# A two-layer graph and expert kernel on one core: the first layer's expert blocks get their first product from seven half-size products as well, alternating with the second product of the block before

## The chip, the cores and the metric

One core of a Trainium2 chip runs the whole program. The metric is the device time of one execution in microseconds (us); the time of a kernel is the median of its runs. TensorE (PE in the profile; PEld is its loading of weights) multiplies, VectorE (DVE), ScalarE (ACT) and GpSimd (POOL) work on tiles, SyncE (SP) issues most of the loads from HBM. Each engine takes its own instructions in order and waits on semaphores for the others.

## The reference

Two layers, each a graph step followed by a mixture of eight experts of which two are taken for each of 3327 tokens with 256 features. The change touches the experts of the first layer only:

```python
def _L0_ffn_ref(x, Wg, bg, W1, b1, W2, b2):
    B, S, D, H, E, K = (8, 8192, 256, 1024, 8, 2)
    gate_scores = jnp.einsum('bsd,ed->bse', x, Wg) + bg
    topk_scores, topk_idx = jax.lax.top_k(gate_scores, K)
    topk_probs = jax.nn.softmax(topk_scores, axis=-1)
    combine = jnp.sum(topk_probs[..., None] * jax.nn.one_hot(topk_idx, E, dtype=x.dtype), axis=-2)
    out = jnp.zeros_like(x)
    for e in range(E):
        h = jax.nn.relu(jnp.einsum('bsd,hd->bsh', x, W1[e]) + b1[e])
        y = jnp.einsum('bsh,dh->bsd', h, W2[e]) + b2[e]
        out = out + combine[..., e:e + 1] * y
    return out
...
x = x + _L0_gnn_ref(_layernorm(x, axis=-1), adj, L0_gnn_W, L0_gnn_b)
x = x + _L0_ffn_ref((_layernorm(x, axis=-1))[None], L0_ffn_Wg, L0_ffn_bg, L0_ffn_W1, L0_ffn_b1, L0_ffn_W2, L0_ffn_b2)[0]
```

All of it is in float32.

## The kernel before

Tokens are sorted by expert into a list in HBM (`xlist0`), each row with its weight and its place. The experts work on this list in blocks that belong to one expert each: `step` handles block t. A usual block has 256 rows (two groups of 128); blocks 12, 17, 22, 27 and a few at the end have 128. Blocks 0 to 7 are planned early; 8 to 29 are always run. Three blocks fit into the six places of the ring in SBUF, two places each: w1, the rows (`xb`) and b1 in the one, w2 and b2 in the other.

What step t does before the change:

- `load` issues the loads of block t+2 on SP, in the order `xlist`, w1 (L1296), b1, w2, b2. The first waits until the place of block t-1 is free, that is until VectorE has done the last L1434 of that block (it reads the rows' weights from `xb`).
- `prepare` has VectorE make four sums of quarters of w2 (L1346 to L1349, 128x512 each) in the tile `gate`.
- `first` computes the hidden tile hT of 1024 x 256 from xT, the block turned to features by rows, and w1: for each of eight chunks of 128 hidden features two matmuls of 128x256 (L1379) into a PSUM bank of pool `psh`, then one ScalarE activation, relu with the bias (L1387).
- `weighed_bias` fills y with the bias by the row's weight (ScalarE, L1364). `turned` transposes block t+1 on TensorE (L1325) and ScalarE copies it (L1329).
- `second_seven` (blocks 3 to 28 of 256 rows) computes the second product as seven products of half-size blocks in place of eight: VectorE makes four sums of quarters of hT (L1370, L1418 to L1420), TensorE multiplies four 128x128 matmuls for each of the seven (L1427), VectorE adds each result, by the row's weight, into the quarters of y it belongs to (L1434), and GpSimd scatters the two halves of y to HBM (L946). The 128-row blocks use `second` (L1476, L1483, L1484).

All matmuls of a block's first product come before those of its second. Which instruction stands where in an engine's queue is decided by a scheduler when the program is built, from the order in the code; within an engine the order is then fixed.

The kernel's PSUM tiles come from three pools: two buffers in `psh`, four in `psy` (second products), two in `pst` (transposes elsewhere in the kernel). `xn` is a work tile with three buffers, used when tokens are routed and between the layers. Elsewhere in the kernel, while the second layer's graph step runs, GpSimd adds tiles of 128x512 in SBUF (L1870) and copies them (L919) while VectorE adds larger tiles (L459) and, from PSUM, L717.

Of the kernel before, what the change touches and what calls it, by code (L numbers as in the profile page):

```python
# [10 lines left out]
F32 = mybir.dt.float32  # L11
# [11 lines left out]
P = 128  # L23
NT = 26
NP = NT * P
D = 256
# [102 lines left out]
def gnn_moe_two_layers(  # L129
# [1086 lines left out]
    def experts(xlist, ys, group, fixed, n_hidden, func, w1T, b1, w2T, b2, copy, order_of_places, kept=None,  # L1216
                seven=None):

# [113 lines left out]
        def halves(a, k, i):  # L1332
            return a[:, k * hc_n // 2 : (k + 1) * hc_n // 2, ts(i, P)]

        def prepare(t):

            if not seven or t not in seven or groups_of(t) < SG:
                return None
            w2 = loaded[t][4]
            flat = gate.rearrange("p e d -> p (e d)")  # L1340
            n = hc_n // 2 * P
            sums = [flat[:, i * n : (i + 1) * n].rearrange("p (c d) -> p c d", d=P) for i in range(4)]
            t1, t3, t2, t4 = sums
            b21, b22 = halves(w2, 1, 0), halves(w2, 1, 1)
            with behind(last_y):
                nc.vector.tensor_tensor(t1, halves(w2, 0, 1), halves(w2, 0, 0), ALU.subtract)  # L1346
                nc.vector.tensor_tensor(t2, b22, t1, ALU.subtract)
                nc.vector.tensor_tensor(t4, b21, t2, ALU.subtract)
                nc.vector.tensor_tensor(t3, b22, halves(w2, 0, 1), ALU.subtract)  # L1349
            tokens_ = [  # L1350
                work.tile([P, DC, 2 * P], F32, name=name, bufs=2).rearrange(
                    "p c (h d) -> p (c h) d", d=P
                )
                for name in ("xnT", "xnT", "h2T", "h2T")
            ]
            return sums, tokens_

# [53 lines left out]
        def second_seven(t, late, hT, sums, y):  # L1411

            (t1, t3, t2, t4), (s1, s2, s3, s4) = sums
            _, xb, _, _, w2, _ = loaded[t]
            index = place_of(t, late)
            a11, a12, a21, a22 = (halves(hT, k, i) for i in range(2) for k in range(2))
            b11, b21, b22 = halves(w2, 0, 0), halves(w2, 1, 0), halves(w2, 1, 1)
            nc.vector.tensor_tensor(s1, a21, a22, ALU.add)  # L1418
            nc.vector.tensor_tensor(s2, s1, a11, ALU.subtract)
            nc.vector.tensor_tensor(s4, a12, s2, ALU.subtract)  # L1420
            ps_x, ps_q, ps_b, ps_z = (
                psy.tile([P, P], F32, name="ps_y", tag="py") for _ in range(4)
            )

# [12 lines left out]

            multiply(ps_x, a11, b11)
            put_in(0, 0, ps_x)
            multiply(ps_q, a22, t4)  # L1440
            put_in(1, 0, ps_q)
            multiply(ps_b, a12, b21)
            put_in(0, 0, ps_b)
            multiply(ps_z, s1, t1)
            put_in(1, 1, ps_z)
            multiply(ps_x, s2, t2, False)
            put_in(0, 1, ps_x)
            multiply(ps_z, s4, b22, False)
            put_in(0, 1, ps_z)
            put(y, index, 0)  # L1450
            multiply(ps_x, s3, t3, False)
            put_in(1, 0, ps_x)
            put_in(1, 1, ps_x)
            put(y, index, 1)

# [47 lines left out]
        def step(late, end=always, place=None, between=None):  # L1503
# [3 lines left out]
            while len(loaded) < min(t + RING // places, end):  # L1507
                load(late)
            if t not in ready:
                ready[t] = turned(loaded[t][1], groups_of(t))  # L1510
# [136 lines left out]
    def count(pan, k, copied):  # L1647
# [9 lines left out]
        xlist0, ys0, "0", FIXED[0], H, AF.Relu, f0_w1T, f0_b1, f0_w2T, f0_b2,  # L1657
        nc.scalar.copy, BLOCKS0, seven=range(3, EARLY + LATE_PAIRS + FIXED[0] - 1),
    )

# [542 lines left out]
```

## Time and profile before

| what | value |
|---|---|
| median of 11 runs (lowest to highest) | 1171.19 us (1168.41 to 1174.14) |
| the profiled execution | 1169.44 us, span 1167.7 us |
| granted TensorE clock | 0.994 |
| TensorE busy, 0 to 200 us | 194.92 us |
| TensorE busy, 200 to 400 us | 200.00 us |
| TensorE busy, 1100 us to the end | 45.17 of 68 us |
| VectorE / ScalarE / GpSimd busy, 500 to 550 us | 24.80 / 18.47 / 7.34 of 50 us |
| first product L1379 x1184 | 253.4 us, 367 ns mean of one |
| second product of 256-row blocks, L1427, five rows of the page's groups | x352 46.5, x352 43.1, three x176 of 23.3 us |
| relu L1387 x282 | 128.5 us, 457 ns mean; 473 ns for 128x256 |
| VectorE sums L1418 x22, 128x512 | 692 ns mean |
| VectorE L1434 x176, 128x128 from PSUM | 348 ns mean |
| GpSimd sum L1870 x12, 128x512 | 1.26 to 4.52 us |

A float32 matmul has two records in the profile (the transposes have one). The records of matmuls that follow each other overlap in the trace (a mean of 367 ns for 1184 records, but 253.4 us busy), so the cost of a matmul is read from the distance between starts. In the page a group's idle time is that of its engine just before its instructions.

### The profile page before, as it was taken

What the parts mean: (1) busy time and instruction counts of PE and PEld (TensorE: products, weight loads), DVE (VectorE), ACT (ScalarE), POOL (GpSimd) and SP (SyncE); (2) the same over time, 40 slices, a digit from 0 to 9 for tenths busy, and PEclk for the clock granted to TensorE, in tenths of its full rate; (3) what the DMA queues carried; (4) which work ended last, traced back from release to release, by engine and by line L of the source; (5) the groups of instructions that cost most, each with busy time, mean ns of one, the idle gap of its engine ahead of it and who ended that gap; (6) DMA issues with size and microseconds to landing.
All of it is one profiled execution on the core that took longest, in us unless ns stands there. A gap on an engine that the chain in (4) does not pass through costs nothing. (4 is left out here: it accounts for less than half of the span.)

```text
span 1167.7 us, 19508 instructions
## 1 busy us (share of the span) xinstructions
PE 1136.4 (97%) x6235; PEld 995.0 (85%) x6235; DVE 838.1 (72%) x2621; ACT 606.0 (52%) x1111; POOL 317.0 (27%) x370
## 2 busy tenths in 40 slices
PE   8999999999999999999999999999999999999983
PEld 7888888888888888889898888888888888888872
DVE  6699999988885555454545569675897887886464
ACT  5689657550323333433333425997797776143331
POOL 2111331342431111111111110011353254465442
PEclk9999999999999999999999999999999999999997
DMA  9996638715467655766675856227347443478686
GB/s 350 189 292 244 234 131 250 260 58 185 141 223 236 222 197 185 246 210 204 206 253 186 318 192 266 85 92 252 129 148 265 165 144 136 144 249 243 223 300 228
DMA packets 123248, 241.68 MB, mean 207 GB/s; under 512 B 24528, under 2 KB 93184, under 8 KB 116224
## 3 DMA queue, kind: packets, MB, share of 16 engines
q1 hardware_dynamic: 108656, 205.59, 53.3%
q0 software_dynamic: 11200, 31.61, 7.4%
q10 hardware_dynamic: 3280, 3.15, 0.8%
q8 instruction: 51, 0.84, 0.3%
q14 instruction: 61, 0.50, 0.1%
HBM read 203.99 MB, written 36.33 MB: 206 GB/s over the span
## 5 line engine op out<-in xcount | busy, mean ns | idle before, releaser
L1387 ACT ACTIVATE pad<-ps_h,ring 128x256 f32<-128x256 f32 (+1 forms) x282 | 128.5, 457 | 284.6 <-PE ps_h L1379 149.6
L1379 PE MATMUL ps_h<-pad,ring 128*128 128x256 f32 (+1 forms) x1184 | 253.4, 367 | 3.1 <-ACT pad L1329 2.7
L1379 PEld LDWEIGHTS ps_h<-pad,ring 128*128 128x128 f32 x1184 | 200.6, 190 | 44.8 <-ACT pad L1387 10.3
L449 PE MATMUL ps_g<-ring,pad 128*128 128x256 f32 x1040 | 235.6, 381 | 0.8 <-DMA ring<-in_adjT 0.8
L449 PEld LDWEIGHTS ps_g<-ring,pad 128*128 128x128 f32 x1040 | 195.4, 190 | 26.0 <-DMA ring<-in_adjT 1.2
L946 POOL DMA_INDIRECT ys<-pad,index x114 | 115.7, 1015 | 361.8 <-DVE pad L1434 223.3
L449 PE MATMUL ps_g<-ring,s 128*128 128x256 f32 x780 | 176.9, 379 | 0.0
L459 DVE TENSOR_TENSOR ring<-ring,ring 128x768 f32<-128x768 f32 (+1 forms) x160 | 167.7, 1091 | 0.0
L449 PEld LDWEIGHTS ps_g<-ring,s 128*128 128x128 f32 x780 | 148.2, 190 | 19.6
L675 ACT ACTIVATE ring<-ring 128x3328 f32<-128x3328 f32 x54 | 160.0, 2976 | 1.4 <-DMA ring<-in_adjT 1.1
L946 POOL DMA_INDIRECT xlist<-xn,rt_idx x104 | 118.9, 1143 | 127.4 <-issue 30.0
L1651 ACT ACTIVATE sign<-ring,below 128x416 bf16<-128x416 f32 x208 | 133.4, 641 | 11.7 <-DMA ring<-in_adjT 5.7
L819 DVE SCALAR_TENSOR_TENSOR rt_product<-xn,gate 128x256 f32<-128x256 f32 x256 | 116.5, 455 | 15.0 <-ACT xn L361 6.2
L1434 DVE SCALAR_TENSOR_TENSOR pad<-ps_y,ring,pad 128x128 f32<-128x128 f32 x176 | 59.2, 348 | 47.3 <-PE ps_y L1427 47.2
L474 PE MATMUL ps_g<-ring,s 128*128 128x256 f32 x312 | 68.8, 380 | 3.2 <-ACT s L361 3.2
L474 PEld LDWEIGHTS ps_g<-ring,s 128*128 128x128 f32 x312 | 59.0, 190 | 11.7 <-ACT s L361 4.1
L756 PE MATMUL ps_g<-s,ring 128*128 128x256 f32 x312 | 69.0, 380 | 0.0
L756 PEld LDWEIGHTS ps_g<-s,ring 128*128 128x128 f32 x312 | 59.0, 191 | 7.7
L1418 DVE TENSOR_TENSOR xnT<-pad 128x512 f32<-128x512 f32 x22 | 15.2, 692 | 59.4 <-ACT pad L1387 59.4
L1476 PE MATMUL ps_y<-ring,pad 128*128 128x256 f32 x224 | 52.4, 380 | 0.0
L1476 PE MATMUL ps_y<-s,pad 128*128 128x256 f32 (+1 forms) x200 | 48.9, 383 | 0.1
L929 POOL COPY xn<-rt_w 128x4 f32<-128x4 f32 x26 | 4.5, 199 | 162.9 <-DVE rt_w L892 162.9
(255 smaller groups left out, 1566.2 us busy)
## 6 DMA issues: line engine op xcount, KB each, us to landing
ring<-in_adjT SPq DMA_DIRECT2D x50, 1664.0 KB, 8.1
ring<-in_f_w1T SPq DMA_DIRECT2D x30, 1024.0 KB, 6.9
ring<-in_f_w2T SPq DMA_DIRECT2D x30, 1024.0 KB, 7.5
ring<-xlist SPq DMA_DIRECT2D x52, 258.0 KB, 3.4
ring<-in_f_w SPq DMA_DIRECT2D x36, 256.0 KB, 3.8
ring<-ys SPq DMA_DIRECT2D x12, 512.0 KB, 5.3
ring<-in_f_b SPq DMA_DIRECT2D x34, 128.0 KB, 8.2
xlist<-h2T SPq DMA_DIRECT2D x16, 257.0 KB, 7.2
```

What stands on the lines that cost most here:

```text
L449: nc.tensor.matmul(ps, lhsT=b[:, c, :], rhs=a[:, c, :], start=(first and c == 0), stop=(c == CJ - 1), skip_group_check=not first,)
L459: nc.vector.tensor_tensor(out[:, part, :], out[:, part, :], other[:, part, :], ALU.add)
L474: nc.tensor.matmul(sums[pan][c], lhsT=s[:, j, ts(c, P)], rhs=piece(pan, j // CJ)[:, j % CJ, :], start=(j == 0), stop=(j == NT - 1),)
L675: last_pass[:] = [nc.scalar.activation(a, a, f)]
L756: nc.tensor.matmul(banks_[it], lhsT=piece(pan, k)[:, c, ts(it, P)], rhs=s[:, j, :], start=(j == 0), stop=(j == NT - 1),)
L819: nc.vector.scalar_tensor_tensor(product, xn, 1.0, gate[:, e, :], ALU.mult, ALU.mult, accum_out=sc[:, e : e + 1],)
L946: d = nc.gpsimd.indirect_dma_start(out=a[:, :], out_offset=bass.IndirectOffsetOnAxis(ap=index, axis=0), in_=rows_, in_offset=None,)
L1379: last_product[:] = [nc.tensor.matmul(ps, lhsT=w1[:, c, ts(hc, P)], rhs=xT[:, c, :], start=(c == 0), stop=(c == DC - 1),)]
L1387: nc.scalar.activation(hT[:, hc, :], ps, func, bias=bb1[:, hc : hc + 1])
L1434: last_y[:] = [nc.vector.scalar_tensor_tensor(part, ps, xb[:, g, WT : WT + 1], part, ALU.mult, ALU.add)]
L1476: last_product[:] = [nc.tensor.matmul(ps, lhsT=hT[:, hc, ts(g, P)], rhs=w2[:, hc, :], start=(hc == 0), stop=(hc == hc_n - 1),)]
L1651: nc.scalar.activation(sign, piece(pan, k)[:, :, ts(i, GROUP)], AF.Sign, bias=below, accum_out=positive[:, pan, i, k : k + 1],)
```

## The change

Blocks 3 to 24 go through a new `piped_step`. For a block of 256 rows from 4 to 24 the first product, too, is made of seven products of half-size blocks: 7 x 4 matmuls of 128x128 (`first_parts`) in place of 16 of 128x256. In step t they are the ones of block t+1, and they alternate with the parts of the second product of block t (`second_parts`, or `single_parts` for a 128-row block). Block t+2 is turned, and its sums are made, in step t as well. Block 3 itself still has the old first product.

- Sums of quarters of w1 (`sum_weights`, 128x512 each): three on GpSimd, one on VectorE, into tiles `xn`, of which all three buffers are taken. Their instructions are L1528 to L1531 of the changed kernel (L1530 is VectorE's).
- Sums of the turned tokens (`sum_tokens`): three on VectorE (L1540, L1543, L1544).
- The seven results pass through three PSUM banks; ScalarE copies three of them into hT, VectorE adds to three quarters there (L1600, L1613, L1622), and relu goes over quarters in sixteen activations of 128x128 (L1590).
- The second product's parts come in another order, and two additions of its last result become one of 128x256 (L1498). The other additions are L1442, the sums of hT are L1447, L1448, L1451 and L1478; the sums of w2 (L1350 in part) are made between the parts.

In the built program, VectorE's L1530 stands ahead of L1613, and the loads of block t+2 are issued at the start of step t, as before.

```diff
-    def prepare(t):
+    def prepare(t, in_turn=False):
...
+        if in_turn:
+            return sums, [lambda q=q: nc.vector.tensor_tensor(*q, ALU.subtract) for q in steps_]
...
+def second_parts(t, late, hT, sums, y, s3_made=False):
...
+    def sums_12():
+        nc.vector.tensor_tensor(s1, a21, a22, ALU.add)
+        nc.vector.tensor_tensor(s2, s1, a11, ALU.subtract)
+    def sum_4():
+        nc.vector.tensor_tensor(s4, a12, s2, ALU.subtract)
...
+    def x_1():
+        multiply(ps_x, a11, b11)
+        if not s3_made:
+            sums_12()
+        put_in(0, 0, ps_x)
+    def q_():
+        multiply(ps_q, a22, t4)
+        put_in(1, 0, ps_q)
+        if not s3_made:
+            put(y, index, 1)
+    def b_():
+        multiply(ps_b, a12, b21)
+        if not s3_made:
+            sum_4()
+        put_in(0, 0, ps_b)
+    def z_1():
+        multiply(ps_z, s1, t1)
+        if not s3_made:
+            nc.vector.tensor_tensor(s3, a11, a21, ALU.subtract)
+        put_in(1, 1, ps_z)
+    def x_2():
+        multiply(ps_x, s2, t2, False)
+        put_in(0, 1, ps_x)
+    def z_2():
+        multiply(ps_z, s4, b22, False)
+        put_in(0, 1, ps_z)
+        put(y, index, 0)
+    def x_3():
+        multiply(ps_x, s3, t3, False)
+        if s3_made:
+            put_in(1, 0, ps_x)
+            put_in(1, 1, ps_x)
+            put(y, index, 1)
+            return
+        both = y[:, 1, :].rearrange("p (h d) -> p h d", d=P)
+        last_y[:] = [nc.vector.scalar_tensor_tensor(
+            both, ps_x.unsqueeze(1).to_broadcast([P, 2, P]), xb[:, 1, WT : WT + 1], both,
+            ALU.mult, ALU.add,
+        )]
+    if s3_made:
+        return [x_1, q_, b_, z_1, x_2, z_2, x_3]
+    return [x_1, b_, z_1, x_2, z_2, x_3, q_]
+weight_sums, token_sums, hidden, ahead_sums = [], {}, {}, {}
+def quarter(w1, k, d):
+    n = n_hidden // 2
+    return w1[:, d, k * n : (k + 1) * n]
+def sum_weights(t):
...
+        weight_sums.extend([tiles[2][:, 0 : 4 * P], tiles[2][:, 4 * P : 8 * P]])
+    s1, s2, s3, s4 = weight_sums[0:4]
+    w1 = loaded[t][2]
+    a11, a12, a21, a22 = (quarter(w1, k, d) for k in range(2) for d in range(2))
+    return [
+        lambda: nc.gpsimd.tensor_tensor(s1, a21, a22, ALU.add),
+        lambda: nc.gpsimd.tensor_tensor(s2, s1, a11, ALU.subtract),
+        lambda: nc.vector.tensor_tensor(s3, a11, a21, ALU.subtract),
+        lambda: nc.gpsimd.tensor_tensor(s4, a12, s2, ALU.subtract),
+    ]
+def sum_tokens(t):
+    xT = ready[t]
+    b11, b12, b21, b22 = (xT[:, d, ts(i, P)] for d in range(2) for i in range(2))
+    t1, t3, t2, t4 = (weight_sums[4 + t % 2][:, ts(i, P)] for i in range(4))
+    both = weight_sums[4 + t % 2][:, 0 : 2 * P].rearrange("p (i d) -> p i d", d=P)
+    nc.vector.tensor_tensor(
+        both, xT[:, :, P : 2 * P], xT[:, 0, :].rearrange("p (i d) -> p i d", d=P), ALU.subtract
+    )
+    nc.vector.tensor_tensor(t2, b22, t1, ALU.subtract)
+    nc.vector.tensor_tensor(t4, b21, t2, ALU.subtract)
+    token_sums[t] = t1, t2, t3, t4
+def first_parts(t):
+    _, _, w1, bb1, _, _ = loaded[t]
+    xT = ready.pop(t)
...
+    def multiply(out, a, b, first=True):
+        for c in range(hn):
+            last_product[:] = [nc.tensor.matmul(
+                out[:, c, :], lhsT=a[:, ts(c, P)], rhs=b, start=(first and c == 0),
+                stop=(c == hn - 1), skip_group_check=True,
+            )]
+    def relu(k, i, src):
+        for c in range(hn):
+            hc = k * hn + c
+            last_hidden[:] = [nc.scalar.activation(
+                hT[:, hc, ts(i, P)], src[:, c, :], func, bias=bb1[:, hc : hc + 1]
+            )]
+    def part1():
+        multiply(bank("b", psh, "ph"), a11, b11)
+        nc.scalar.copy(c11, ps["b"])
+    def part2():
+        multiply(bank("a", pst, "pt"), a12, b21)
+        nc.vector.tensor_tensor(c11, c11, ps["a"], ALU.add)
+        relu(0, 0, c11)
+    def part3():
+        multiply(ps["b"], s2, t2, False)
+        nc.scalar.copy(c12, ps["b"])
+    def part4():
+        multiply(bank("z", pst, "pt"), s1, t1)
+    def part5():
+        multiply(ps["b"], s3, t3, False)
+        nc.scalar.copy(c22, ps["b"])
+        nc.vector.tensor_tensor(c22, c22, ps["z"], ALU.add)
+    def part6():
+        multiply(ps["b"], a22, t4, False)
+        relu(1, 1, c22)
+        relu(1, 0, ps["b"])
+    def part7():
+        multiply(ps["z"], s4, b22, False)
+        nc.vector.tensor_tensor(c12, c12, ps["z"], ALU.add)
+        relu(0, 1, c12)
+    return [part1, part2, part3, part4, part5, part6, part7]
+def piped_step(t, late, place):
+    nothing = lambda: None
+    more = t + 1 in piped
+    if t not in hidden:
+        ahead_sums[t] = prepare(t)[0]
+        hidden[t] = first(ready.pop(t), loaded[t][2], loaded[t][3], groups_of(t))
+        if more:
+            turn(t + 1, place)
+    sums = ahead_sums.pop(t, None)
+    nexts, weights_ = [nothing] * 4, [nothing] * 4
+    if more:
+        made = prepare(t + 1, True)
+        if made:
+            ahead_sums[t + 1], nexts = made
+        if t + 2 in piped and groups_of(t + 2) == SG:
+            weights_ = sum_weights(t + 2)
+    if sums:
+        y = weighed_bias(t)
+        second_ = second_parts(t, late, hidden.pop(t), (sums, tokens_of()), y)
+    else:
+        second_ = [lambda q=q: q and q() for q in spread(single_parts(t, late, hidden.pop(t)))]
+    first_ = spread(first_parts(t + 1)) if more else [nothing] * 7
+    if not more:
+        turn(t + 1, place)
+    def after_first(i):
+        if i == 3:
+            weights_[0]()
+            weights_[1]()
+        if i == 4:
+            if t + 2 in piped:
+                turn(t + 2, place)
+        if i == 5:
+            weights_[2]()
+        if i == 6:
+            weights_[3]()
+    def after_second(i):
+        if i in (2, 3, 5, 6):
+            nexts[{2: 0, 3: 1, 5: 3, 6: 2}[i]]()
+    for i in range(7):
+        if first_[i]:
+            first_[i]()
+        after_first(i)
+        if second_[i]:
+            second_[i]()
+        after_second(i)
+def turn(t, place=None):
+    ready[t] = turned(loaded[t][1], groups_of(t), place)
+    if t in piped and groups_of(t) == SG:
+        if not weight_sums:
+            for q in sum_weights(t):
+                q()
+        sum_tokens(t)
...
+        if t in piped:
+            piped_step(t, late, place)
+            return
...
+    piped=range(3, EARLY + LATE_PAIRS + FIXED[0] - 5),
```

`single_parts` is the old second product of a 128-row block in four parts of two matmuls, and `spread` lays four parts over the seven places. `s3_made` is true only where `second_seven` still calls the parts, after block 24.

## The prediction

> **What bounds the kernel now.** First the page, for the engine that is never idle; then the busy times of the stage that the change touches (blocks 3 to 24 of layer 0's experts); then one step of it in order of time; then what the step's loads take; last, from another stage, how VectorE and GpSimd get on together.
>
> ```profile
> span 1167.7 us, 19508 instructions
> PE 1136.4 (97%) x6235; PEld 995.0 (85%) x6235; DVE 838.1 (72%) x2621; ACT 606.0 (52%) x1111; POOL 317.0 (27%) x370
> ```
> ```profile
> 346.00:640.00 294.00, 293.80 (x1974) 262.13 (x1973) 158.72 (x372) 110.81 (x247) 44.30 (x42) 1.00 0.66 218
> ```
> The columns of the second are window, length, then busy us of PE, PEld, DVE, ACT and POOL, clock, DMA share, GB/s. TensorE is busy for 293.80 of 294 us at the full clock; the others wait for it. So time is won here by taking work off TensorE, and lost as soon as TensorE waits for one of the others.
>
> ```profile
> 358.38 7.16 PE L1379 MATMUL ps_h<-pad,ring 128*128 128x256 f32 x32
> ...
> 359.32 0.38 SPq L1289 DMA_DIRECT2D ring<-xlist  x1
> 359.94 0.37 SPq L1296 DMA_DIRECT2D ring<-in_f_w1T  x1
> ...
> 365.38 0.60 PE L1325 MATMUL ptb<-ident,ring 128*128 128x128 f32 x4
> 365.82 1.06 PE L1427 MATMUL ps_y<-ring,pad 128*128 128x128 f32 x8
> ...
> 372.07 1.25 PE L1379 MATMUL ps_h<-pad,ring 128*128 128x256 f32 x5
> ```
> A pair step: first product 7.00 us (358.38 to 365.38, 16 matmuls in 32 records), the turning of the next block 0.44, seven second products to 372.07, so 6.25 or 0.89 each; 13.69 in all. The load of the block two further on is issued 0.94 into the step, when the last L1434 of the step before has let go of its place.
>
> ```profile
> DMA to landing us min/median/max: 6.0/6.3/6.5
> ```
> ```profile
> DMA to landing us min/median/max: 6.9/7.6/8.2
> ```
> Issue to landing of w1 (L1296), 358 to 445 us and 520 to 640 us, where the trace has it. The longer ones stand by 128-row blocks, whose step is 7.6 us, so that two loads overlap. Today a w1 has a whole step to spare after landing.
>
> ```profile
> 866.79 6.40 DVE L459 TENSOR_TENSOR ring<-ring,ring 128x1024 f32<-128x1024 f32 x4
> 867.25 1.90 POOL L1870 TENSOR_TENSOR x<-x,xn 128x512 f32<-128x512 f32 x1 [2.12 <-ACT xn L361]
> 869.10 1.33 POOL L919 COPY xn<-xn 128x512 f32<-128x512 f32 x1
> 870.39 1.98 POOL L1870 TENSOR_TENSOR x<-x,xn 128x512 f32<-128x512 f32 x1
> 872.32 1.34 POOL L919 COPY xn<-xn 128x512 f32<-128x512 f32 x1
> 873.11 0.41 DVE L717 TENSOR_TENSOR h2T<-h2T,ps_g 128x256 f32<-128x256 f32 x1
> ```
> ```profile
> 824.37 3.83 DVE L459 TENSOR_TENSOR ring<-ring,ring 128x1024 f32<-128x1024 f32 x4
> 824.81 4.52 POOL L1870 TENSOR_TENSOR x<-x,xn 128x512 f32<-128x512 f32 x1 [6.71 <-ACT xn L361]
> ```
> Four additions of two SBUF tiles take VectorE 3.83 us when GpSimd is held off, and 6.40 when GpSimd's come in between; GpSimd's, held off, ends 1.13 us after VectorE's last (828.20 to 829.33). Where they take turns, a 128x512 sum on GpSimd costs VectorE about 1.1. An addition with an operand from PSUM (L717, 873.11) keeps its 0.41 beside a GpSimd copy.
>
> [...] The row at 824.81 differs: GpSimd came during VectorE's first addition and was held off through three more. If that were usual here, VectorE would lose nothing, and the sum would be rival (a)'s.
>
> **The change, part by part.** Call the seven first products of block t+1 P1 to P7 and the seven second products of block t X1 to X7; TensorE goes P1 X1 P2 X2 and so on, with the turning of block t+2 after P5.
>
> TensorE: 28 half-width matmuls for 16 of full width. The form is that of L1427, so 6.25 for 7.00: 0.75 won for each pair block from 4 to 24 but 12, 17 and 22, that is 18, **13.5 us**. A clear step is then 12.94. Alternating costs nothing by the rows: where L1379 and L1476 take turns today (469.8 to 472.6 us) no gap stands between.
>
> ScalarE: eight activations of 473 ns become sixteen of 128 columns and three copies. Two L1364 that follow each other take 0.89 at 497 ns each, so they start 0.39 apart; taking 128 columns as 0.1 us less, sixteen cost about 4.3, and the copies (L1329, 128x512: 0.58) 1.7. With the bias and the copy of the turned tile about 8 us in 12.94: hidden.
>
> VectorE: 128x512 tiles start 0.60 apart (454.90, 455.50, 456.10 us), 128x128 ones 0.26. Added are three sums into the hidden tile (1.8), one difference of w1 (0.6) and three of the tokens (0.8); the last two L1434 become one. About 7 us become 10 of 12.94. That fits on average, but it is in order, and two things now stand in its queue.
>
> First, the w1 difference waits for the landing of a w1 issued in the same step, and by the order of instructions it stands ahead of the sum into c22. Behind that sum are eight activations (2.4 us), and behind those P1 of the next step, which takes their bank. P5, which also frees the old difference, ends at 8.0; w1 lands at 0.55 (last L1442 of the step before) + 0.75 (to L1296) + 6.7 (between the two landing rows, nearer to undisturbed steps) = 8.0. So on time, barely.
>
> Second, GpSimd gets three sums a step, 1.13 each, two of them waiting for the same w1. Today it only issues scatters. From the landing on VectorE has 4.15 us of work to the end of the block's y (difference 0.6, c22 0.6, tokens 0.8, L1442 and its pair 0.9, gate 0.6, c12 0.6). One 1.13 falls half under c22, whose other operand is in PSUM like L717's, the other between two token sums: 1.6 more, 5.75. The next load starts only then. The loop is 0.75 + 6.7 + 5.75 = 13.2 against 12.94: it slips 0.25 a step, and TensorE feels the slip only after some five; steps with no new w1 (10, 15, 20, 23) make it up. I put all this, and the unfilled step 24, where X3 waits 0.3 for its sum, at **1.5 us**; bounds 0 (no clash) and 10 x 0.9 = 9 (landing 7.3).
>
> **The three 128-row blocks** (12, 17, 22) are where it breaks. Step 11 is TensorE work of 7 x 0.89 + 4 x 0.89 + 0.44 = 10.25 us. Its w1 (block 13) lands at 8.0, and all three GpSimd sums run at once, against the difference, three token sums and a gate sum. In turns: difference 8.0 to 8.7, GpSimd to 9.8, first token sum 10.2, GpSimd 11.3, second 11.55, GpSimd 12.7, then third token sum, pair, gate sum, L1442: 14.15. So the load for step 12 starts 3.9 us into that step, whose TensorE work is 6.25 + 3.5 + 0.44 = 10.2.
>
> In step 12 VectorE still owes three gate sums (to 6.0), then P2's sum (6.7); four activations (7.9); the copy of P3 (8.5). P5 needs that copy and would have begun at 6.2: 2.35 lost. w1 of block 14 lands at 3.9 + 0.75 + 6.7 = 11.35; difference to 11.95, c22 to 12.65, eight activations to 15.1: P1 of the next step begins at 15.1 and not at 10.2. That is **4.9 us**; with GpSimd first 6.0. I take 5.5, three times: **16.5**. Bounds: 1.85 each without clashes (step 11 ends its y 3.1 after 8.0, w1 lands at 8.4 of step 12, activations end at 12.05), and 6.7 with a landing of 7.3.
>
> Queues: behind the w1 wait on GpSimd stand the two scatters of y; their buffer is wanted two steps on, over 12 us later, so nothing waits. SP issues as many loads as before, in the same order. TensorE's turning of block t+2 waits for xlist, 3.4 after an issue at 0.7, well before 8.0. Cover that can go: the copies of P1 and P3 hide under three slots (2.67); if lost, each costs up to 0.6.
>
> Sum: -13.5 + 16.5 + 1.5 = +4.5. The profiled execution took 1169.44 us (span 1167.7 and 1.7 around it), 1.75 under the median of 1171.19. So 1173.9 for such an execution, **1175.7** for the median.
>
> **The rivals.** (a) Faster: the clash is smaller than I lay it out. For: the row at 824.81, where GpSimd alone waited, and w1 may land in 6.0 with the scatters moved out of its way. Against: in the rows from 866.79 on they take turns. Time: -13.5 + 3 x 1.85 + 0.5 = -7.5, so 1163.7; with nothing lost at all 1157.7.
>
> (b) Slower throughout: the load loop becomes the bound of every step, not only at the 128-row blocks. It decides from 0.75 + landing + 5.75 > 12.94, clearly so from a landing of 7.3, which the rows from 520 us on reach. Then 13.8 a step: ten steps x 0.86, less some 2 for the first slips, 6.6; 128-row blocks 3 x 6.7 = 20; -13.5 + 6.6 + 20 = +13, 1184. Against: those landings belong to loads that overlap, and the changed kernel's are over 10 us apart.
>
> (c) No difference: stalls and savings cancel, within 2.3 us (0.2%, about what a measurement of this kernel tells from no change). It needs 12 us of stalls, 4 at each 128-row block.
>
> That the change does less than it says, a half-width matmul not costing half, is excluded by L1427, which is that form already.
>
> **How the numbers follow.** Forecast (4.5 slower; from 1.5 to 9) 0.42, of which 0.05 falls within 0.2%; (a) 0.33; (b) 0.15; (c) 0.10. So faster 0.33, same 0.05 + 0.10 = 0.15, slower 0.37 + 0.15 = 0.52. The time is the forecast's, 1175.7. Its own range is 1172 to 1181. The range for 8 in 10 reaches past (a)'s centre and to (b)'s: 1162 to 1184.
>
> **What would show it.** Right: TensorE idle or waiting some 5 us at each of the three 128-row blocks, ended by ScalarE's L1590 (P1's bank) and by the copy of P3; VectorE waiting for w1 at L1530; two-input sums of 0.69 us at up to 1.8 beside L1528 and L1529; pair steps of 12.9 to 13.2 elsewhere. Wrong on the clash: L1447, L1448 and L1350 all at 0.69. Wrong on the landing: no wait at L1530. The forecast falls as a whole if steps 11 and 12 together take no longer than the same blocks' 13.69 + 7.6 = 21.3 us of today.

## The result and the profile after

| | median (lowest to highest) | to the kernel before, 95% interval |
|---|---|---|
| kernel before | 1170.92 us (1168.41 to 1175.31) | |
| changed kernel | 1185.74 us (1179.42 to 1192.35) | 1.0129 (1.0117 to 1.0141) |

The change makes the kernel 14.8 us slower; 4.5 were forecast. Each of the later sets of runs was made on one chip with the kernel before timed beside it, and the chips differ: where the kernel before took 1187 us, the change cost 1.0060 (1.0038 to 1.0081), where it took 1173, 1.0091 (1.0059 to 1.0122). So ratios are taken within one chip, and times are not compared across chips.

The head of the page of the changed kernel, in an execution of 1191.64 us; the kernel before had 1136.4 us of TensorE in a span of 1167.7:

```profile
span 1189.5 us, 20695 instructions
...
PE 1134.9 (95%) x6667; PEld 1015.3 (85%) x6667; DVE 927.7 (78%) x2728; ACT 653.1 (55%) x1309; POOL 396.7 (33%) x424
```

This execution is 5.9 us over the median of its kernel, so its waits are longer than usual ones; all sums below are of it. TensorE was busy 1.5 us less and the span is 21.8 longer. A clear pair step, in order of time (start, us, engine, line, tile), goes from one turning to the next in 12.94 us, with a first and a second product by turns; it took 13.69 before:

```profile
364.05 0.60 PE L1325 MATMUL ptb<-ident,ring 128*128 128x128 f32 x4
364.48 1.06 PE L1435 MATMUL ps_y<-ring,h2T 128*128 128x128 f32 x8
365.38 1.06 PE L1582 MATMUL ps_f<-xn,ring 128*128 128x128 f32 x8
...
376.10 1.06 PE L1582 MATMUL ps_f<-xn 128*128 128x128 f32 x8
376.99 0.60 PE L1325 MATMUL ptb<-ident,ring 128*128 128x128 f32 x4
```

And w1 (L1296), issue to landing. The trace has 8 of the 23 landings from 352 to 660 us, and these took less than before; where it has none, the first use of a w1 by an engine that waited for it is taken as its landing in what follows:

```profile
DMA to landing us min/median/max: 5.2/5.9/6.3
```

The busy times by stretch (window, length, then busy us of PE, PEld, DVE, ACT and POOL, clock, DMA share, GB/s) show it for the stage that the change touches and, below, for three stretches of 14 us in it:

```profile
338.20:667.50 329.30, 307.10 (x2493) 295.39 (x2493) 260.98 (x545) 162.24 (x454) 128.06 (x99) 0.98 0.62 206
444.00:458.00 14.00, 11.95 (x93) 11.79 (x92) 12.29 (x22) 6.85 (x21) 6.33 (x5) 0.88 0.63 208
514.00:528.00 14.00, 11.52 (x89) 11.36 (x89) 11.37 (x22) 6.04 (x19) 4.45 (x4) 0.88 0.61 190
654.00:668.00 14.00, 11.22 (x58) 9.44 (x58) 5.87 (x22) 3.66 (x8) 1.92 (x2) 0.88 0.49 180
```

The first line goes from the turning (L1325) of block 3 to that of block 27, the first behind the branch that follows the stage: 329.3 us, where the kernel before took 311.1 (337.4 to 648.5). VectorE's work grew from 171.76 us to 260.98. In the three short stretches TensorE has a wait and the granted clock is 0.88: the clock is full but for 3.41 us, which run at half. The kernel before has no such drop ahead of 1152 us.

TensorE's waits from 353 to 672 us, in the view of waits (us in total, times, longest):

```profile
PE ps_f L1582 <- POOL xn L1531: 4.9, 3, 1.6
PE ps_f L1582 <- issue: 4.5, 2, 2.5
PE ps_f L1582 <- DVE pad L1613: 3.4, 5, 1.6
PE ps_f L1582 <- ACT pad L1605: 3.0, 3, 1.1
PE ps_h L1385 <- DVE pl_flag L1161: 2.8, 1, 2.8
PE ps_f L1582 <- DVE xn L1543: 2.5, 1, 2.5
PE ps_y L1435 <- DVE pad L1442: 0.9, 1, 0.9
```

22.0 us in all; from the distances between matmuls some 4 more are in gaps under 0.35 us. With 1.7 us for each clock drop (3.41 us at half) that is 31.1, less the 13.5 won is 17.6; the stage grew by 18.2. What follows asks where the waits come from. Three kinds are seen.

**One late w1.** A timeline (start, us, engine, line, tile; in brackets the idle time before and what ended it) of steps 14 and 15. w1 was issued at 503.48:

```profile
503.48 0.37 SPq L1296 DMA_DIRECT2D ring<-in_f_w1T  x1
...
511.97 0.69 DVE L1530 TENSOR_TENSOR xn<-ring 128x512 f32<-128x512 f32 x1 [1.90 <-DMA ring<-in_f_w1T]
512.01 1.78 POOL L1528 TENSOR_TENSOR xn<-ring 128x512 f32<-128x512 f32 x1 [7.21 <-DMA ring<-in_f_w1T]
...
512.58 0.68 DVE L1613 TENSOR_TENSOR pad<-pad,ps_f 128x512 f32<-128x512 f32 x1
...
515.37 0.97 POOL L946 DMA_INDIRECT ys<-pad,index  x1 [0.16 <-DVE xn L1543]
...
516.01 2.19 DVE L1350 TENSOR_TENSOR gate<-ring 128x512 f32<-128x512 f32 x1
...
516.36 1.29 POOL L1531 TENSOR_TENSOR xn<-ring,xn 128x512 f32<-128x512 f32 x1
...
518.13 0.68 DVE L1622 TENSOR_TENSOR pad<-pad,ps_f 128x512 f32<-128x512 f32 x1
...
518.84 1.28 ACT L1590 ACTIVATE pad<-pad,ring 128x128 f32<-128x128 f32 x4 [3.25 <-DVE pad L1622]
...
520.02 0.90 ACT L1370 ACTIVATE pad<-ring,ring 128x256 f32<-128x256 f32 x2
...
520.82 0.57 ACT L1596 COPY pad<-ps_f 128x512 f32<-128x512 f32 x1
...
521.48 0.79 PE L1582 MATMUL ps_f<-xn 128*128 128x128 f32 x4 [2.48 <-issue]
```

It landed after 8.5 us (5.9 is the median of those landings that the trace has). VectorE, GpSimd and the sum into c22 (L1613) began there. Then VectorE's gate sum at 516.01 took 2.19 us and not 0.68: GpSimd was busy with a scatter (L946, to 516.34) and went on with its third weight sum (L1531, to 517.65), and VectorE's sum ended 0.55 behind that. A scatter alone held none of VectorE's sums up here: 39 of them with two inputs (128x512) ran beside an L946 without a weight sum and kept 0.68 to 0.69 us. So P7's sum (L1622) came at 518.13, then four activations, the two biases (L1370), and only then the copy of the next P1 (L1596) that P3 needs: TensorE stood still for 2.48 us, at the pair step behind the late load. The wait of 2.05 us at 453.60 has the same history, with a w1 issued at 436.59 and used from 444.09 on. The 2.5 that ended with L1543 stand at block 3, where the alternation starts: VectorE was held 3.8 us at L1530 by the w1 of block 4, and the token sums behind it came late. That w1 took a usual 6.4 us to land, but was issued 3.77 us behind the turning of block 3 (1.80 in run 5, which has no such wait).

**The 128-row blocks.** Behind each there are two waits in the block's own two steps (three at block 17) and another of 1.8 us (5.4 in all) at the P3 of the step that follows, here at 492.24:

```profile
490.18 1.28 POOL L1531 TENSOR_TENSOR xn<-ring,xn 128x512 f32<-128x512 f32 x1
...
490.78 0.89 ACT L1370 ACTIVATE pad<-ring,ring 128x256 f32<-128x256 f32 x2
...
491.58 0.56 ACT L1596 COPY pad<-ps_f 128x512 f32<-128x512 f32 x1
...
492.24 1.02 PE L1582 MATMUL ps_f<-xn 128*128 128x128 f32 x7 [1.64 <-POOL xn L1531]
```

The view puts it down to GpSimd's L1531, but that was done at 491.46. The copy of P1 ended at 492.14, and P3 began 0.1 later: it was ScalarE's queue once more (run 8 shows it).

**The branch.** Ahead of the first block behind the stage, TensorE waits for the flag that chooses how the program goes on:

```profile
656.06 0.17 PE L959 MATMUL pc<-cum,ones_sq 128*128 128x8 bf16 x1
...
657.96 0.15 DVE L1161 CAST pl_flag<-pl_ok 128x1 int32<-128x1 f32 x1
...
659.00 1.62 PE L1385 MATMUL ps_h<-s,ring 128*128 128x256 f32 x3 [2.77 <-DVE pl_flag L1161]
```

The flag's little product (L959) now stands behind the last X7 on TensorE, and seven small vector instructions follow it. In the kernel before the same vector work was done at 469 us, in the middle of the stage.

### The profile page after: what moved, and what is told of

The parts are those of the page before. It is cut to its first block, busy times and chain, and to the rows that moved or that the text cites. A ratio compares the mean times of both kernels' runs of the same rounds, so it can differ in the third digit from the quotient of the medians.

```text
span 1189.5 us, 20695 instructions
## 1 busy us (share of the span) xinstructions
PE 1134.9 (95%) x6667; PEld 1015.3 (85%) x6667; DVE 927.7 (78%) x2728; ACT 653.1 (55%) x1309; POOL 396.7 (33%) x424
## 5 line engine op out<-in xcount | busy, mean ns | idle before, releaser
L946 POOL DMA_INDIRECT ys<-pad,index x114 | 118.5, 1040 | 203.6 <-DVE pad L1741 51.9
L946 POOL DMA_INDIRECT xlist<-xn,rt_idx x104 | 116.1, 1116 | 126.2 <-issue 37.6
L1393 ACT ACTIVATE pad<-ps_h,ring 128x256 f32<-128x256 f32 (+1 forms) x114 | 51.7, 455 | 122.4 <-PE ps_h L1385 95.4
L1385 PE MATMUL ps_h<-pad,ring 128*128 128x256 f32 (+1 forms) x512 | 113.4, 371 | 3.5 <-ACT pad L1329 3.4
L1590 ACT ACTIVATE pad<-pad,ring 128x128 f32<-128x128 f32 x216 | 69.0, 390 | 79.3 <-DVE pad L1600 33.3
L1385 PEld LDWEIGHTS ps_h<-pad,ring 128*128 128x128 f32 x512 | 90.5, 194 | 19.5 <-ACT pad L1329 3.8
L1582 PE MATMUL ps_f<-xn 128*128 128x128 f32 x432 | 59.2, 282 | 15.0 <-POOL xn L1531 4.9
L1582 PEld LDWEIGHTS ps_f<-xn 128*128 128x128 f32 x432 | 54.2, 197 | 17.4 <-issue 7.5
L1442 DVE SCALAR_TENSOR_TENSOR pad<-ps_y,ring,pad 128x128 f32<-128x128 f32 x138 | 47.1, 346 | 20.4 <-PE ps_y L1435 19.4
L1528 POOL TENSOR_TENSOR xn<-ring 128x512 f32<-128x512 f32 x18 | 28.3, 1571 | 96.3 <-DMA ring<-in_f_w1T 77.7
```

What stands on the lines that cost most here:

```text
L946: d = nc.gpsimd.indirect_dma_start(out=a[:, :], out_offset=bass.IndirectOffsetOnAxis(ap=index, axis=0), in_=rows_, in_offset=None,)
L1385: last_product[:] = [nc.tensor.matmul(ps, lhsT=w1[:, c, ts(hc, P)], rhs=xT[:, c, :], start=(c == 0), stop=(c == DC - 1),)]
L1393: nc.scalar.activation(hT[:, hc, :], ps, func, bias=bb1[:, hc : hc + 1])
L1582: last_product[:] = [nc.tensor.matmul(out[:, c, :], lhsT=a[:, ts(c, P)], rhs=b, start=(first and c == 0), stop=(c == hn - 1), skip_group_c ...
L1590: last_hidden[:] = [nc.scalar.activation(hT[:, hc, ts(i, P)], src[:, c, :], func, bias=bb1[:, hc : hc + 1])]
```

## The experiments

The measure for the stage is the time from the turning of block 3 to that of block 27, in the profiled execution. Theory A says that the clash of GpSimd's sums with VectorE's makes the waits, theory D that it is the landing of w1, since VectorE has no time to make up a late one; B and C are named where they come.

**Runs 1 to 4, on a chip with 1187.6 us for the kernel before.**

Run 1, the flag written ahead of the steps:

```diff
...
+    first_usual = usual(
+        [(BEGUN, late[4][:, E : 2 * E])],
+        [(late[5][0:1, :], FIXED[0]), (most_all, TOPK + 0.5)],
+        early=True,
+    )
     layer0.steps_to(late, layer0.tiers_done)
...
-    first_usual = usual(
-        [(BEGUN, late[4][:, E : 2 * E])],
-        [(late[5][0:1, :], FIXED[0]), (most_all, TOPK + 0.5)],
-    )
+    first_usual = first_usual()
```

> Only the vector work that gives the branch's flag (from the small product L959 to the cast L1161) is written ahead of the steps instead of behind them. In the trace of the changed kernel TensorE stands still for 2.77 us before L1385 at 659.00, behind that cast, and runs at half clock for 3.41 us around it (some 1.7 us). Theory A (the flag is late because the order of the program puts its product behind the last X7): both go, 2.8 + 1.7 = 4.5 us less than the changed kernel, so 1.009 of the kernel before; L1161 stands hundreds of us earlier and no idle of TensorE over 1 us is left between 652 and 668. Rival (the branch itself, or the loads behind it, would hold the first product as long): no more than 1 us less.

Measured: 1.0028 (1.0007 to 1.0049); the stage 313.4 us, no wait at the branch. The changed kernel was not timed on this chip; another chip of the same speed gave it 1.0060 (run 5), so 3.8 us less, though the intervals touch and the stage is no shorter than run 5's 312.9: it has a wait of 2.5 us and two drops of the clock that run 5's profile has not. Theory A's account of the flag holds; what it is worth is taken up with runs 14 and 15.

Run 2, the 128-row blocks left out of the alternation:

```diff
                 if more:
+                    if weight_sums:
+                        for q in sum_weights(t + 1):
+                            q()
                     turn(t + 1, place)
...
-        piped=range(3, EARLY + LATE_PAIRS + FIXED[0] - 5),
+        piped=[t for t in range(3, EARLY + LATE_PAIRS + FIXED[0] - 5) if t not in (12, 17, 22)],
```

> Blocks 12, 17 and 22 (128 rows) and the first products of the pair blocks behind them are left as in the kernel before; blocks 4 to 11, 14 to 16, 19 to 21 and 24 keep the seven products and the alternation, 15 of the 18. Theory A (the waits arise where two 128-row steps shorten the time that a load has, and run on from there): the savings are 15 x 0.75 = 11.25; what stays is the 2.65 at block 3, the 4.5 at the branch and 1 to 2 of small waits, so 2 to 4 us under the kernel before, ratio 0.997 to 0.998. Rival B (VectorE and the load loop bind every step, the 128-row blocks or not): waits of 10 us or more stay, ratio 1.003 or above.

Measured: 0.9989 (0.9968 to 1.0010), stage 308.4 us (its end taken at the same turning), and one wait in the list:

```profile
PE ps_h L1385 <- DVE pl_flag L1161: 2.8, 1, 2.8
```

So with pair blocks alone the alternation runs almost free of waits. It took 5.0 us less than run 1 on the same chip, though run 1 has no wait at the branch: the 128-row blocks cost more than the three savings that they take along. Rival B falls.

Run 3, GpSimd's sums left out after the first block:

```diff
...
-            return [
+            full = [
...
+            if len(once) == 0:
+                once.append(t)
+                return full
+            return [lambda: None, lambda: None, full[2], lambda: None]
```

> The three sums of w1 on GpSimd are made for the first block alone; the later blocks use the old sums, so their products are of other numbers but of the same size. [...] Rival B (the landing of w1, which L1530 still waits for, sets the waits): at most the 5.4 that end with L1531 go, ratio 1.008 or above.

Measured: 1.0163 (1.0142 to 1.0184) as a whole, which says nothing: the kernel leaves out sums that its result needs, and other numbers can send other tokens to other experts in the second layer. The stage can be read, as its blocks are planned ahead of it: 308.8 us, against 312.9 for the changed kernel on such a chip (run 5), and waits of 0.35 us or more sum to 6.9 and not 14.4; 2.9 of the 6.9 are the branch. By theory A the three waits of 1.8 us behind the 128-row blocks (5.4), the two of 2.2 and 2.65 at the P3 of steps 10 and 15 and their drops of the clock were to go, 13 us; 4.1 came. Landings of 7.5 to 8.0 us (issued at 344.05, 373.43, 386.48 and 536.40) stand in this profile too, and only the last was followed by a wait of TensorE of 2 us or more. Five pair steps (64.8 us), of the changed kernel and then of this one, show the clash itself (window, length, busy us as above):

```profile
367.20:432.00 64.80, 64.38 (x575) 64.06 (x574) 61.10 (x113) 37.63 (x108) 32.78 (x25) 1.00 0.64 214
```

```profile
367.20:432.00 64.80, 64.80 (x583) 64.80 (x582) 52.84 (x117) 38.31 (x110) 9.59 (x10) 1.00 0.63 206
```

VectorE was busy 61.10 us in the changed kernel and 52.84 without GpSimd's sums: the clash costs VectorE 8.26 us in five steps, 1.65 a step, and leaves it 0.74 us a step. The two windows do not hold quite the same work (113 and 117 instructions of VectorE, and a wait of TensorE of 0.42 us in the first); the window of run 11 further down, with 117, gives 1.45 a step. The wait of 2.4 us that stayed is at a 128-row block (block 17).

Run 4, the alternation alone, with first products of full width and no sums for them (the flag early):

```diff
...
-            if groups_of(t) < SG:
+            if True:
+                w = groups_of(t) * P
+
                 def some(at):
                     for hc in range(at, at + 2):
-                        ps = psh.tile([P, P], F32, name="ps_h", tag="ph")
+                        ps = psh.tile([P, w], F32, name="ps_h", tag="ph")
...
-                if t + 2 in piped and groups_of(t + 2) == SG:
+                if False:
...
-            if t in piped and groups_of(t) == SG:
+            if False:
...
```

> The alternation alone: first products as in the kernel before (16 of full width) but in four parts between the second products, no sums of w1 or of tokens; the flag early as in the first run. Theory A (alternating costs TensorE nothing; all loss comes from the sums and what waits for them): within 2 us of the kernel before, ratio 0.998 to 1.002. Rival (alternating itself costs, by waits for PSUM banks or by a clash of the order with ScalarE's queue): 0.3 us or more at each of 21 blocks, ratio 1.005 or above.

Measured: 0.9988 (0.9973 to 1.0002); clear pair steps of 13.60 us, where the kernel before has 13.69. Alternating costs TensorE nothing, as theory A and the forecast had it.

**Runs 5 to 8, on a chip with 1187.3 us for the kernel before.** The changed kernel itself:

> The changed kernel itself once more, beside the other three on one chip, since the first four runs were on a chip on which the kernel before took 1187.6 us, 17 more than when the change was timed. All theories: 1.011 to 1.015 of the kernel before on the same chip. By theory A (TensorE's waits come from GpSimd's sums, and drop the clock where they are long) the profile has 20 to 30 us of waits between blocks 3 and 25, and half clock for 3.4 us behind each wait over 2 us; their places may differ from the first profile's, since they hang on when w1 lands.

Measured: 1.0060 (1.0038 to 1.0081), below what was expected. The stage took 312.9 us, with waits of 14.4 us of 0.35 or more, where 20 to 30 were expected, and no clock drop. (The profiled execution is 5.3 us under the median here, and was 5.9 over it on the first chip.) A w1 that landed after 7.3 us stands in step 12, and a wait of 1.9 followed in that step.

Run 6, the runs of pair blocks alone and the early flag (the diffs of runs 1 and 2 together):

> Seven first products for the runs of pair blocks alone (as in the second run) and the flag early (as in the first). Theory A: the savings of the second run, and the 2.8 + 1.7 us at the branch less: 6 to 7 us under the kernel before, ratio 0.994 to 0.995. Rival B (what is won ahead of the branch is lost behind it, because the loads of the outputs or the scatters end last there): ratio 0.998 or above, with a new wait behind 640 us.

Measured: 0.9969 (0.9948 to 0.9990), 2.4 us better than run 2 was on its chip, less than expected: the profile has one wait of 2.5 us with a clock drop, at a pair step (461.09), where none was foreseen.

Run 7, the difference of w1 on GpSimd:

```diff
-                lambda: nc.vector.tensor_tensor(s3, a11, a21, ALU.subtract),
+                lambda: nc.gpsimd.tensor_tensor(s3, a11, a21, ALU.subtract),
```

> The difference of w1 (L1530) goes from VectorE to GpSimd, so that VectorE never waits for a w1; GpSimd then makes four sums a step. Theory C (VectorE waiting at L1530 with the sum into c22 and the rest of the block queued behind is the heaviest part of the waits): the wait of 2.65 at block 3 and those of P6 (L1582 ended by L1613) go, 6 to 10 us less than the changed kernel. Theory A (the clash of GpSimd's sums with VectorE's is the heaviest): a fourth sum clashes too and the last sums come 1.3 later, so nothing is won: within 3 us of the changed kernel or slower, with more waits that end with GpSimd's sums.

Measured: 1.0073 (1.0050 to 1.0096), and the stage 322.1 us with three clock drops:

```profile
PE ps_f L1582 <- POOL xn L1531: 7.1, 3, 2.7
PE ps_f L1582 <- issue: 3.6, 3, 1.3
PE ps_f L1582 <- ACT pad L1605: 3.5, 3, 2.2
PE ps_h L1385 <- DVE pl_flag L1161: 2.8, 1, 2.8
```

The waits for VectorE's sum into c22 (L1613) are gone (they are P7's, by the tiles pad and xn, and not P6's), and those for GpSimd's last sum are longer: theory C (VectorE's own wait at L1530 is the heaviest part) falls. The work behind a late w1 is the same, whichever engine has it.

Run 8, the weighed biases behind the copy of P1:

```diff
-                nc.scalar.copy(c11, ps["b"])
+                last_copy[:] = [nc.scalar.copy(c11, ps["b"])]
...
-                y = weighed_bias(t)
+                y = blk("narrow", SG * D).rearrange("p (g d) -> p g d", d=D)
...
+                if i == 0 and sums:
+                    at = last_copy if first_[2] and len(last_copy) else last_hidden
+                    with behind(at):
+                        for g in range(SG):
+                            nc.scalar.activation(
+                                y[:, g, :], loaded[t][5], AF.Copy, scale=loaded[t][1][:, g, WT : WT + 1]
+                            )
...
```

> On ScalarE the two weighed biases (L1370, 0.89 us) stand behind the copy of P1 and not ahead of it. Theory A: P3 of steps 10 and 15 waited for that copy, which stood behind four activations and the two biases; the copy comes 0.8 earlier, so each such wait is 0.8 shorter and may fall under the 2 us from which the clock drops: 1.6 to 5 us less than the changed kernel. Rival (the copy is late because the activations are, and the first L1442, which needs the biases, now holds VectorE instead): within 1 us of the changed kernel.

Measured: 1.0064 (1.0042 to 1.0087), no gain. In the trace the three waits of 1.8 us behind the 128-row blocks are 1.0 now, which shows that the copy did end them, but there are other waits (2.4 us in all for L1442, not 0; 2.7 for the copy of P3, not 0.9 as in run 5). The rival holds.

**Runs 9 to 11, on a chip with 1173.5 us.** The kernel before, for its profile:

> The kernel before, for a profile of it on the same chip as the runs beside it: the change cost 14.8 us on the chip of the first timing (1.0129) and 6.4 on the second (1.006), and both theories need to know from which stage the difference comes. Theory A (the waits depend on when single w1 loads land, and the first profile of the changed kernel had four late ones): the stage from block 3 to the branch takes the same 311 us in the kernel before on either chip, and the chip differs elsewhere. Rival (this chip is slower for the kernel before in that very stage): more than 314.

Measured: 0.9994 (0.9979 to 1.0009), stage 311.1 us, as on the first chip.

Run 10, w1 a step earlier:

```diff
...
+            d, w1 = w1_loads.pop(t) if t in w1_loads else load_w1(t, e)
...
             loaded.append((d, xb, w1, bb1, w2, bb2))
+            if t + 1 in piped and t + 1 - RING // places in hidden:
+                w1_loads[t + 1] = load_w1(t + 1, expert(t + 1, late, [SP]))
...
```

> The w1 of blocks 7 to 24 is loaded a step earlier: issued behind the other loads of the block before, into the place that the first product of the block three before has left. Nothing else is changed; GpSimd's sums still clash with VectorE's. Theory D (what failed is the landing: a w1 that lands 7 us or more after its issue, or two loads in a short step, leaves VectorE, with no slack, behind for more than a step): L1530 and L1528 wait for no w1; of the waits of TensorE from block 6 to 24 less than 3 us are left, no clock drop but at the branch; 8 to 12 us less than the changed kernel, ratio 0.996 to 0.999. Theory A alone (the clash is enough, w1 early or not): two thirds of the waits stay, ratio 1.003 or above.

Measured: 0.9962 (0.9940 to 0.9985), stage 308.3 us, and these waits of TensorE (lines are 9 further down here: L1591 is L1582, L1622 is L1613, L1552 is L1543, L1539 is L1530):

```profile
PE ps_h L1394 <- DVE pl_flag L1161: 2.8, 1, 2.8
PE ps_f L1591 <- DVE pad L1622: 2.1, 3, 1.1
PE ps_f L1591 <- DVE xn L1552: 1.3, 1, 1.3
PE ps_f L1591 <- issue: 0.6, 3, 0.2
```

6.8 us are left of 22.0, and 2.8 of them are the branch; no clock drop in the stage. By the distances of matmuls the waits of 0.35 us or more, without the branch, sum to 5.2 us and not 21.8; 1.45 of the 5.2 are at block 3. VectorE's waits for w1, which were to go, are a quarter of what they were; the changed kernel's, from the same window, stand first (us in total, times, longest):

```profile
DVE xn L1530 <- DMA ring<-in_f_w1T: 25.0, 8, 5.4
```

```profile
DVE xn L1539 <- DMA ring<-in_f_w1T: 6.3, 3, 2.4
```

All of GpSimd's sums are still there. With the early flag added (run 11):

> The run before and the early flag together. Theory D: another 3 to 4.5 us less than with the early w1 alone: 10 us or more under the kernel before, ratio 0.990 to 0.993. Rival B (a time won ahead of the branch is lost to loads and scatters behind it): ratio as with the early w1 alone, a wait of 2 us or more for a DMA behind the branch.

Measured: 0.9965 (0.9949 to 0.9981), no better in time, though the stage took 302.6 us and the last matmul came 3.4 us sooner. In five clear pair steps VectorE is nearly as busy as in the changed kernel (61.10 there):

```profile
362.20:427.00 64.80, 64.80 (x583) 64.80 (x582) 60.07 (x117) 38.33 (x110) 32.00 (x26) 1.00 0.68 214
```

So the clash is all there, and TensorE hardly waits: theory A alone falls. With run 3, where the clash was gone and the loads as late as ever, it takes both: a VectorE that is full, and a load that comes late.

**Runs 12 to 15, on a chip with 1172.9 us.** The changed kernel a third time:

> The changed kernel beside the three others on one chip. Theory D (waits of TensorE follow single late landings of w1, since VectorE has under 0.8 us a step to make them up): 1.005 to 1.014 of the kernel before, and in the profile each wait of 2 us or more at P3 of a pair step comes one step behind a w1 that landed over 7 us from its issue.

Measured: 1.0091 (1.0059 to 1.0122), stage 328.2 us. A w1 that landed after 7.75 us (issued at 424.50) is followed by a wait of 2.3 us and a clock drop at the P3 of the next pair step, 441.73; the w1 of block 4 (7.4 us) by 3.5 us at block 3.

Run 13, w1 behind w2 in its block's loads:

```diff
+            if t < 5 or t not in piped:
+                d = nc.sync.dma_start(
+                    out=w1, in_=w1T[ds(e, 1), :, :].rearrange("o (c p) h -> p (o c) h", p=P)
+                )
...
+            if t >= 5 and t in piped:
+                d = nc.sync.dma_start(
+                    out=w1, in_=w1T[ds(e, 1), :, :].rearrange("o (c p) h -> p (o c) h", p=P)
+                )
             loaded.append((d, xb, w1, bb1, w2, bb2))
```

> The w1 of blocks 5 to 24 is issued last of its block's loads, behind b1, w2 and b2, and not second; nothing else is changed. By the first profile the old issue to landing is 5.9 us, the four issues take about 2, and w2, which would now be ahead of it, lands 8.0 after its own issue: w1 lands 3 to 4 us later than in the changed kernel. Theory D: the loop of issue, landing and VectorE's work (0.75 + 9.5 + 5.75 = 16.0) is over the 12.94 of TensorE's work, so each of some 15 pair steps grows by 2 to 3.3 us: 30 to 50 us over the changed kernel, ratio 1.03 to 1.06, with L1582 waiting in every step. [...]

Measured: 1.0398 (1.0380 to 1.0415), 36 us over the changed kernel on the same chip. w1 is issued 1.8 us later and takes 9.8 to land instead of 5.9, so it lands 5.7 later, more than was expected; the stage took 359.9 us with eight clock drops, and TensorE waits for w1 itself (L1587 is L1582):

```profile
PE ps_f L1587 <- issue: 18.5, 8, 3.1
PE ps_f L1587 <- DMA ring<-in_f_w1T: 13.8, 8, 3.5
```

Runs 14 and 15, those with w1 a step earlier once more, without and with the early flag:

> The kernel with w1 a step earlier once more. Theory D: 0.994 to 0.999 of the kernel before, 9 to 20 us under the changed kernel on the same chip, no wait of TensorE over 2 us but the one at the branch.

> The same with the early flag. If the flag is worth its wait in the trace (2.9 us): 0.991 to 0.996 and 2 to 4 us under the run before it. Rival (the last loads and scatters of the kernel take up what is won): within 1 us of the run before it.

Measured: 0.9984 (0.9972 to 0.9996) and 0.9951 (0.9932 to 0.9969). On this one chip the changed kernel stands at 1183.41 us, w1 a step earlier at 1170.82 and the early flag besides at 1167.14: 16.3 us less than the changed kernel and 5.8 less than the one before. The flag is worth 3.7 us here and nothing in runs 10 and 11, where the profiled execution gave 3.6 us back behind its last matmul (span less last matmul 22.4 us against 18.8, in the last scatter and load). Whether that is chance is not settled.

## Why the prediction was wrong

**TensorE's saving (-13.5): right.** Clear pair steps take 12.94 us, as forecast; alternating cost nothing (run 4: 13.60 us a step against 13.69).

**The clash: right in size.** VectorE does wait for w1 at L1530 (eight times from 353 to 640 us, 25.0 us in all), and 1.6 us of VectorE's time a step were forecast, 1.45 to 1.65 are measured. Two-input sums of 0.68 us take up to 2.2, above the 1.8 named: two of L1350 took 2.21 and 2.19 us (448.12 and 516.01), each where a weight sum of GpSimd follows right behind a scatter. In the row at 516.01 VectorE's sum is recorded 0.35 us ahead of GpSimd's (516.36) and yet ended 0.55 behind it. Why it lost is not shown.

**The 128-row blocks (+16.5): the place was right, the size a little high, the path in part another.** Their waits, with the one at the P3 behind, were 3.4, 6.0 and 3.8 us by the distances of matmuls, 13.2 in all. The forecast let each loss end with the copy of P3 and then with the activations that free P1's bank (L1590); no wait of TensorE in the list ends with L1590. They ended with the copy of P3, as forecast; with the sum into c22 itself, which P7 waits for, as it writes the bank that the sum reads; and with the copy of the next P1, which the forecast had taken for hidden: the 1.8 us behind each block are the cover that it named as one that could go, at three times the price named (0.6).

**The +1.5 for the load loop in the pair steps: the step that failed.** The forecast took one landing time, 6.7 us, let the loop slip by 0.25 a step and had steps with no new w1 make it up. The median landing, 5.9, was better than that, but three took 7.4 to 8.5 (issued at 436.59, 503.48 and 533.65; the third adds to the 6.0 of block 17), and VectorE's spare time of 0.74 us a step can't take up 2 us. The first two came through to TensorE within a step or two: 2.2 us behind the first, 0.5 and 2.65 behind the second. With 0.6 in step 6, behind no late w1, that is 6.0 us instead of 1.5, and two of the three drops of the clock below came right behind the two long waits. An average of the loop was used where its worst turn decides. Runs 10 and 13 show that it is the landing, on a VectorE as full as this (run 3): a step earlier takes 12.6 us off on one and the same chip (run 14 against 12), at the 128-row blocks too; 5.7 us later adds 36.

**Not in the sum at all:** 2.65 us at block 3, where the alternation starts with a load that was issued late; 2.8 us at the branch, since the flag's work came to stand behind X7 through a change that doesn't touch it (why the order came out so is not shown); and three drops of the clock, 1.7 us each. With 13.2, 6.0 and the 13.5 won this comes to 16.2 of the 18.2 us that the stage grew; the rest is in small gaps.

**The rivals.** (b), slower throughout by the loop, named landings of 7.3 us and a time of 1184, 1.7 under the result. But its mechanism, steps of 13.8 us everywhere, is not what happened: clear steps take 12.94 to 12.96, and what was lost came singly. That its time was near is luck. It was thought less likely because its landings belonged to loads that overlap; they occur singly too. (a) is excluded, and so is (c).

What stays open: why one w1 takes 5.2 us and the next 8.5. The loads of a block are all issued on SP (w2's megabyte 1.2 us behind w1), and in the slow one of 503.48 the last issue of the block took 3.27 us, but in that of 436.59 it took 0.55. Why the loss differs from chip to chip, 1.006 to 1.013, was not tried; with one profile for each chip, and executions of the changed kernel that lie up to 13 us apart (the table of the result), the number of late loads can't be held against it.

## What to carry to other kernels

When a change fills an engine nearly up (VectorE here to 94% of the step), cost the loads that it waits for by their slowest landing and not by the median: VectorE had 0.74 us a step left here, and a w1 came 2.6 us later than the median. Before thinning the engine's work, look whether the load can be issued earlier: w1's place had been free for a step, and using that brought 12.6 us with no work taken away. And look for instructions that the change moves without touching them, such as the flag of a later branch.

## What the hardware showed that was not expected

Whether a wait of TensorE is followed by a lower clock did not go by the wait's length alone. In the profile of the changed kernel the granted clock is half three times between 337 and 667 us, from 453.66, 521.92 and 658.46 on, for 3.41 us each, at waits of 2.05, 2.48 and 2.77 us. A wait of 2.49 us that ended at 359.36 was followed by no such drop. The expectations of runs 5 and 8 take it to come from 2 us of wait on; this one does not fit.

The three drops start 68.26 and 136.54 us apart, which is 20 and 40 times 3.413. Cut into stretches of 3.413 us from there, this profile has 2.05, 2.48 and 2.23 us of idle time of TensorE in the stretches right ahead of the three drops, and at most 1.64 in any other from 337 to 667 us; a cut at 358.09 divides the wait of 2.49 into 1.21 and 1.27. That wait cost nothing more, and the one of 2.05 at 453.60 cost 1.7 us on top. What in the hardware decides it is not shown.
